# Two lookup layers with 15 of 16 centroid rows in the table products, the spare matrix in a tile of its own

## The chip, the cores and the metric

The kernel runs on one core of one Trainium2 chip. The metric is the device time of one execution in microseconds (us); before, the median of three runs is 3843.47 us (3841.17 to 3844.94). The engines of the core have program counters of their own: TensorE (PE) multiplies matrices and loads weights (PEld), VectorE (DVE), ScalarE (ACT) and GpSimd (POOL) work elementwise, and SyncE (SP) only issues DMAs. They meet through semaphores.

## The reference

Input `x` is 32 images of 1024 channels and 14x14 pixels, fp32. The model's first layer is group norm followed by three lookup layers with batch norm between them; its second is a linear attention with a depthwise convolution. A lookup layer replaces each group of input values by softmax weights over 16 centroids and sums table rows with these weights:

```python
def _amm(patches, centroids, lut, inv_temp):
    ...
    scores = 2.0 * jnp.einsum('blcs,cks->blck', v, centroids) - jnp.sum(centroids * centroids, -1)[None, None]
    attn = jax.nn.softmax(scores * inv_temp, axis=-1)
    out = jnp.einsum('blck,cko->blo', attn, lut)
...
out = _amm(x, c1_centroids, c1_lut, c1_invt)
out = jax.nn.relu(_bn(out, bn1_g, bn1_b))
out = _amm(_extract3x3(out, 1), c2_centroids, c2_lut, c2_invt)
out = jax.nn.relu(_bn(out, bn2_g, bn2_b))
out = _amm(out, c3_centroids, c3_lut, c3_invt)
```

Layers 1 and 2 (the first two lookups) each have 256 codebooks of 16 centroids, so 4096 table rows, and 256 output channels. The 16 weights of a codebook add up to 1. A table whose rows have all had one row of the codebook subtracted gives outputs that differ by a constant per channel, and the batch norm that follows removes such a constant.

## The kernel before

The images go in 16 pairs of 392 tokens. Layers 1 and 2 run over 128 units each: 16 pairs times 8 blocks of 32 codebooks. A unit's weights lie in a tile `t` of 128 partitions by 4 matrices `j` by 416 columns, of which 392 are tokens; a matrix holds 8 codebooks of 16 rows. `units` (L624) is the loop of both layers. Iteration i issues, in this order, the scores and exponentials of unit i + ahead, the 32x32 transposes of the unit before it (`token_major`, L564), `softmax` of unit i + 2 (L576), whatever `side` has for this iteration, and the table products of unit i (`lut`, L631). `ahead` is 4 in layer 1 and 3 in layer 2, and `ahead + 2` tiles `t` go round.

For a unit, PE computes four scores (L779; in layer 2 eight, L896 and L905, from patches and from the padded image), ACT exponentiates them into `t` (L557), DVE transposes `t` into `tt` (L569), in layer 1 Pool first adds the two halves of the 16 (L572), DVE sums (L586), inverts (L588) and transposes back into `r` (L594), Pool multiplies `t` by `r` (L595), and PE multiplies the unit's four matrices by the two halves of the output channels (eight products, L639), adding up over the eight units of a pair in PSUM. Each product is two records in the profile (fp32).

The order of each engine's instructions is that of the program: the whole part stands in a manual schedule. SP issues in order too. It loads in layer 1 the images (L247, a pair 17 iterations ahead of its eight units) and, at the start, eight tables of 512 KB (L237), nine small constants (L182) and the centroids of layers 2 and 3 (L518, L531, L536). A DMA takes one of eight semaphores in turn and is not issued before the last DMA on that semaphore has landed. In layer 2, ACT normalises a pair into `pad` (L813), SP stores it to DRAM three times shifted (`h1d`, L824), and loads for each group of four units 12 patch pieces (L844, `load_patches`, 4 matrices by 3 taps), a group ahead, all at the group's first unit. The tables of layer 2 are loaded as the last units of layer 1 leave their places, and those of layer 3 likewise.

The group norm of a coming pair stands in `side` of layer 1: sums on DVE (L271), means on PE (L281), and a power on Pool (L299).

A second copy of the layers, `layers(True)`, is run only where sums overflow; it is not executed with these inputs.

Of the kernel before, what the change touches and what calls it, by code (L numbers as in the profile page):

```python
# [150 lines left out]
def conv_preact_kernel(ctx: ExitStack, tc: tile.TileContext, a: dict, out: bass.AP):  # L151
# [207 lines left out]
    def score_biases(ps_tr, pool, tmp, i, raw, rows, groups, mask, per, order=None):  # L359
# [44 lines left out]
    lut1_rows = lambda b: a["lut1"][b * 512 : (b + 1) * 512].rearrange("(s q) w -> q s w", q=P)  # L404


    lut2_rows = lambda b: a["lut2"].rearrange("(h j b q) w -> h b q j w", h=2, j=4, q=P)[
        b // 4, b % 4
    ]
# [78 lines left out]
    def layers(exact, early=None):  # L488
# [87 lines left out]
        def softmax(pool, u, t, tt, tv):  # L576

            tf = t.rearrange("p j n -> p (j n)")
            n = tf.shape[1]
            if exact:  # L580
                mx = pool.tile([P, n // KC], F32, tag="mx", name="mx", bufs=1)
                nc.vector.tensor_reduce(mx, tv, AX.X, ALU.max)
                nc.vector.tensor_tensor(tv, tv, bc(mx, 2, KC), ALU.subtract)
                nc.scalar.activation(tt, tt, AF.Exp)
            sm = pool.tile([P, n // KC], F32, tag="sm", name="sm")
            nc.vector.tensor_reduce(sm, tv, AX.X, ALU.add)  # L586
            rc = pool.tile([P, n // KC], F32, tag="rc", name="rc")
            nc.vector.reciprocal(rc, sm)  # L588
            if exact:
                nc.vector.tensor_tensor(tv, tv, bc(rc, 2, KC), ALU.mult)  # L590
                nc.vector.transpose(tf, tt)
                return
            r = pool.tile([P, n], F32, tag="r", name="r")
            nc.vector.transpose(r, bc(rc, 2, KC))  # L594
            nc.gpsimd.tensor_tensor(tf, tf, r, ALU.mult)  # L595
            nc.scalar.activation(sm, sm, AF.Copy, accum_out=added[:, u : u + 1])  # L596
# [26 lines left out]

        def units(ahead, ts, pool, luts, score, bias, dst, stats, side, last, halve=False):  # L624
# [6 lines left out]
            def lut(u):  # L631
# [5 lines left out]
                order = [(h, j) for h in range(2) for j in range(4)]  # L637
                for h, j in order if b == 7 else sorted(order, key=lambda k: k[1]):
                    nc.tensor.matmul(  # L639
                        po[h],  # L640
                        luts[b][:, j, h * P : (h + 1) * P],
                        ts[u % len(ts)][:, j, :N2],
                        start=(b == 0 and j == 0),
                        stop=(b == 7 and j == 3),
                    )
# [6 lines left out]
            for i in range(-ahead, n):  # L652
# [8 lines left out]
                if 0 <= u < n:  # L661
                    softmax(pool, u, ts[u % len(ts)], *tts.pop(u))
# [12 lines left out]
        with ExitStack() as s:  # L675
# [55 lines left out]
            luts2 = []  # L731

            def next_lut(b):
                return lambda: luts2.append(load_lut(b, lut2_rows(b)))
# [5 lines left out]
            at(40, masks2)  # L740
            for b in range(7):
                at(8 * (NP - 1) + b + 1, next_lut(b))
# [3 lines left out]
            luts = [load_lut(b, lut1_rows(b)) for b in range(8)]  # L746
            if not exact:
                masks()
                load_consts(True)
            for i in (2, 3):  # L750
                load_raw(i)
            load_raw2()
# [20 lines left out]
            def score1(u):  # L773
# [13 lines left out]
                luts,  # L787
# [8 lines left out]
            next_lut(7)()  # L796
# [3 lines left out]
        with ExitStack() as s:  # L800
            once = s.enter_context(tc.tile_pool(name="p2c", bufs=1))
            st = s.enter_context(tc.tile_pool(name="p2tt", bufs=1 if exact else 2))
            luts, luts3 = luts2, []
# [33 lines left out]
            def load_patches(n, b0=0, m=4):  # L837
                p, h = divmod(n, 2)
                for j in range(4):
# [10 lines left out]

            store_pair(0, 0)
# [34 lines left out]
            def score2(u):  # L886
# [3 lines left out]
                if g == 0 and n + 1 < 2 * NP:  # L890
                    load_patches(n + 1)
# [24 lines left out]
            def side2(i):  # L916

                p = {1: 1}.get(i + ahead, (i + ahead + 9) / 8)
                if p in range(1, NP):
                    for h in range(2):  # L920
                        store_pair(int(p), h)
                if i == 60:
# [5 lines left out]
            def next_lut3(b):  # L928
# [10 lines left out]
                luts,  # L939
# [888 lines left out]
```

## Time and profile before

| what | value |
|---|---|
| median of three runs | 3843.47 us |
| the profiled execution, its own time | 3843.16 us |
| its span | 3841.0 us |
| PE busy | 3721.5 us, 97% |
| DVE busy | 3001.9 us, 78% |
| POOL busy | 2302.9 us, 60% |
| ACT busy | 1688.2 us, 44% |
| table products of layers 1 and 2 (L639) | 4096 records, 1417.9 us |
| first and last table product of layer 1 | start at 40.0, end at 860.5 us |
| first and last table product of layer 2 | start at 895.2, end at 1897.8 us |

Busy times are of one execution. The group lines give line, engine, operation, output and input, count, busy time, mean length of one in ns, and the idle time before them with what ended it. A window's line gives, for a stretch of the span, its length and each engine's busy time with the number of instructions, then PE's clock, the busy share of the DMA engines, and GB/s. A timeline's line gives start, length, engine, line, operation and tiles.

### The profile page before, as it was taken

What the parts mean: (1) busy time and instruction counts of PE and PEld (TensorE: products, weight loads), DVE (VectorE), ACT (ScalarE), POOL (GpSimd) and SP (SyncE); (2) the same over time, 40 slices, a digit from 0 to 9 for tenths busy, and PEclk for the clock granted to TensorE, in tenths of its full rate; (3) what the DMA queues carried; (4) which work ended last, traced back from release to release, by engine and by line L of the source; (5) the groups of instructions that cost most, each with busy time, mean ns of one, the idle gap of its engine ahead of it and who ended that gap; (6) DMA issues with size and microseconds to landing.
All of it is one profiled execution on the core that took longest, in us unless ns stands there. A gap on an engine that the chain in (4) does not pass through costs nothing. (4 is left out here: it accounts for less than half of the span.)

```text
span 3841.0 us, 45969 instructions
## 1 busy us (share of the span) xinstructions
PE 3721.5 (97%) x16467; PEld 2085.5 (54%) x16467; DVE 3001.9 (78%) x4281; ACT 1688.2 (44%) x3851; POOL 2302.9 (60%) x1338
## 2 busy tenths in 40 slices
PE   8999999999999999999999999998999999999998
PEld 5555555554555545555444444444666666666665
DVE  8999999978888888888733333332699999999996
ACT  4555555533333333333212221121766776667764
POOL 6999999974444444444321111111788888878886
PEclk9999999999999999999999999999999999999999
DMA  3111101015343424343111110012222223322221
GB/s 117 34 35 34 33 19 34 17 45 121 67 96 71 92 53 94 70 91 74 44 39 47 39 39 26 32 39 97 65 79 84 83 85 91 85 81 84 83 80 34
DMA packets 219107, 243.17 MB, mean 63 GB/s; under 512 B 24368, under 2 KB 216752, under 8 KB 218872
## 3 DMA queue, kind: packets, MB, share of 16 engines
q1 hardware_dynamic: 218296, 240.02, 23.4%
q8 instruction: 132, 2.16, 0.3%
q14 instruction: 103, 0.84, 0.1%
q10 hardware_dynamic: 576, 0.15, 0.0%
HBM read 163.55 MB, written 76.56 MB: 63 GB/s over the span
## 5 line engine op out<-in xcount | busy, mean ns | idle before, releaser
L595 POOL TENSOR_TENSOR t<-t,r 128x1664 f32<-128x1664 f32 (+1 forms) x284 | 1064.5, 3748 | 1187.9 <-DVE r L594 1150.7
L639 PE MATMUL po<-t,lut 128*128 128x392 f32 x4096 | 1417.9, 499 | 0.5 <-POOL t L595 0.5
L639 PEld LDWEIGHTS po<-t,lut 128*128 128x128 f32 x4096 | 759.7, 190 | 626.7 <-issue 123.2
L557 ACT ACTIVATE t<-sc,cbias 128x392 f32<-128x392 f32 (+1 forms) x1136 | 579.8, 593 | 1031.6 <-PE sc L905 646.2
L1338 PE MATMUL mm<-y,lut 128*128 128x392 f32 x2048 | 717.4, 497 | 3.4 <-DVE q L1355 3.2
L1004 PE MATMUL po<-t,lut 128*128 128x448 f32 x1792 | 682.2, 541 | 1.7 <-issue 1.7
L569 DVE STREAM_TRANSPOSE tt<-t 128x1664 f32<-128x1664 f32 (+1 forms) x284 | 544.3, 1916 | 168.1 <-ACT t L557 167.9
L594 DVE STREAM_TRANSPOSE r<-rc 128x1664 f32<-128x1664 f32 (+1 forms) x284 | 546.6, 1925 | 21.3 <-DVE rc L588 0.9
L1560 DVE SCALAR_TENSOR_TENSOR pa<-y,lepe_w,pa 128x406 f32<-128x406 f32 x900 | 541.2, 637 | 19.4 <-PE pa L1542 16.3
L1004 PEld LDWEIGHTS po<-t,lut 128*128 128x128 f32 x1792 | 339.1, 190 | 341.6 <-issue 341.4
L1338 PEld LDWEIGHTS mm<-y,lut 128*128 128x128 f32 x2048 | 373.3, 189 | 253.5 <-issue 10.6
L1013 DVE BATCH_NORM_STATS2 stats<-o 128x6 f32<-128x448 f32 x112 | 68.9, 617 | 487.5 <-ACT o L1012 487.5
L586 DVE TENSOR_REDUCE sm<-tt 128x104 f32<-128x832 f32 (+2 forms) x284 | 423.1, 1490 | 5.4
L572 POOL TENSOR_TENSOR tt<-tt 128x832 f32<-128x832 f32 x128 | 248.1, 1939 | 7.8 <-DVE tt L569 7.8
L1012 ACT COPY o<-po 128x448 f32<-128x448 f32 x112 | 59.0, 528 | 425.4 <-PE po L1004 381.1
L588 DVE RECIPROCAL rc<-sm 128x104 f32<-128x104 f32 (+1 forms) x284 | 229.5, 808 | 9.8
L896 PE MATMUL sc<-patch,cw 64*128 64x392 f32 x1024 | 211.9, 520 | 3.8 <-DMA patch<-h1d 2.4
L596 ACT ACTIVATE sm<-sm 128x104 f32<-128x104 f32 (+1 forms) x284 | 86.1, 303 | 177.2 <-DVE rc L588 177.0
L1523 POOL TENSOR_TENSOR qr<-qr,zb 128x784 f32<-128x784 f32 x64 | 117.8, 1852 | 65.5 <-DMA zb<-zd 65.3
L896 PEld LDWEIGHTS sc<-patch,cw 64*128 64x128 f32 x1024 | 90.5, 186 | 116.2 <-issue 73.7
L1347 ACT ACTIVATE e<-mm,kbd 128x392 f32<-128x392 f32 x128 | 74.3, 580 | 167.0 <-PE mm L1338 165.8
L1191 ACT ACTIVATE w<-x,tb,gn_a 128x196 f32<-128x196 f32 x248 | 128.2, 517 | 29.0 <-DVE x L1205 13.0
(179 smaller groups left out, 3996.4 us busy)
## 6 DMA issues: line engine op xcount, KB each, us to landing
patch<-h1d SPq DMA_DIRECT2D x248, 162.8 KB
x<-in_x_dram SPq DMA_DIRECT2D x32, 784.0 KB
o3d<-o SPq DMA_DIRECT2D x14, 1792.0 KB
x<-in_x_dram SPq DMA_DIRECT2D x64, 392.0 KB
out_dram<-x SPq DMA_DIRECT2D x64, 392.0 KB
o<-o3d SPq DMA_DIRECT2D x62, 392.0 KB
h1d<-pad SPq DMA_DIRECT2D x96, 225.0 KB
patch<-h1d SPq DMA_DIRECT2D x124, 108.5 KB
```

What stands on the lines that cost most here:

```text
L557: nc.scalar.activation(t[:, j, : sc.shape[1]], sc, AF.Identity if exact else AF.Exp, bias=bias[:, j : j + 1],)
L569: nc.vector.transpose(tt, tf)
L572: nc.gpsimd.tensor_tensor(tv[:, :, :8], tv[:, :, :8], tv[:, :, 8:], ALU.add)
L586: nc.vector.tensor_reduce(sm, tv, AX.X, ALU.add)
L588: nc.vector.reciprocal(rc, sm)
L594: nc.vector.transpose(r, bc(rc, 2, KC))
L595: nc.gpsimd.tensor_tensor(tf, tf, r, ALU.mult)
L639: nc.tensor.matmul(po[h], luts[b][:, j, h * P : (h + 1) * P], ts[u % len(ts)][:, j, :N2], start=(b == 0 and j == 0), stop=(b == 7 and j == 3),
L896: nc.tensor.matmul(sc, w8[r, 8 * h + 4 * (j // 2) + g], grid(pbuf[n % NPB][r, j // 2, g]), start=True, stop=False,)
L1004: nc.tensor.matmul(po, luts[g][:, m * P : (m + 1) * P], t3[h][:, g % 4, :], start=(g == 0), stop=(g == 7),)
L1338: nc.tensor.matmul(pv(), w[kt][:, m0 : m0 + P], ywin(p, first + kt), start=(kt == 0), stop=(kt == 3),)
L1560: nc.vector.scalar_tensor_tensor(acc, neighbours(p, c, offset(k)), lw[:, c, k : k + 1], acc, ALU.mult, ALU.add,)
```

## The change

In layers 1 and 2 a group of four units has 16 matrices. The first matrix of the group's first unit is the spare one: it is no longer multiplied. In the other 15, the last row of each codebook is given up (`packed_lut`, `last_rows`): Pool subtracts the codebook's last table row from the whole table block (`less`), and the freed places, partitions 15, 31, ..., 127, take rows of the spare matrix, table and weights alike (15 matrices times 8 places for 8 codebooks times 15 rows). `softmax` writes the spare matrix to a tile `spares` of 128x392, by a second multiplication on Pool, and `spare_rows` copies its rows by DMA, 8x392 each, into `t`: three copies for the first unit of a group, four for each other.

The table is loaded as before (`own`), then its 8 foreign rows (`others`), and into a second tile `d` the last rows, each broadcast over its codebook's 16 places, with the foreign codebooks' last rows at their places. In layer 1 `d` is room in `out1` that is not yet written; in layer 2 it is one of two tiles `drop`, whose next load follows the subtraction. The subtractions of layer 1 stand in iterations -3 to 4, with the loads of a block one to three iterations earlier; in layer 2 they stand in iterations -2 to 5, each with its last foreign load just before it and the load for two blocks later just after.

The small constants and the centroids of layers 2 and 3, loaded at the start before, move to iteration 16 of layer 1 (`later`). `load_patches` issues 6, 3 and 3 pieces at the first three units of a group in place of 12 at the first.

```diff
--- before.py
+++ after.py
@@ -401,12 +401,50 @@
         return bias, biases
-    lut1_rows = lambda b: a["lut1"][b * 512 : (b + 1) * 512].rearrange("(s q) w -> q s w", q=P)
-    lut2_rows = lambda b: a["lut2"].rearrange("(h j b q) w -> h b q j w", h=2, j=4, q=P)[
-        b // 4, b % 4
-    ]
+    lut1_tiles = a["lut1"].rearrange("(b j c k) w -> b j c k w", j=4, c=8, k=KC)
+    lut2_tiles = a["lut2"].rearrange("(h j b c k) w -> h b j c k w", h=2, j=4, c=8, k=KC)
+    def unit_rows(layer, b):
+        return lut1_tiles[b] if layer == 1 else lut2_tiles[b // 4, b % 4]
+    def packed_lut(layer, b):
+        rows, spare = unit_rows(layer, b), unit_rows(layer, b - b % 4)[0]
+        j0 = 0 if b % 4 else 1
+        k0 = 4 * (b % 4) + j0 - 1
+        v = weights[b].rearrange("p (s w) -> p s w", s=4)
+        def own():
+            nc.sync.dma_start(v[:, j0:], rows[j0:].rearrange("j c k w -> (c k) j w"))
+        def others():
+            nc.sync.dma_start(v[15::16, j0:], spare[:, k0 : k0 + 4 - j0])
+        return v, own, others
+    def last_rows(d, layer, b):
+        rows, spare = unit_rows(layer, b), unit_rows(layer, b - b % 4)[0]
+        j0 = 0 if b % 4 else 1
+        v = weights[b].rearrange("p (s w) -> p s w", s=4)
+        d = d.rearrange("p (s w) -> p s w", s=4)
+        for j in range(j0, 4):
+            nc.sync.dma_start(d[:, j], rows[j][:, 15:].to_broadcast([8, KC, W]))
+        def others():
+            nc.sync.dma_start(d[15::16, j0:], spare[:, 15:].to_broadcast([8, 4 - j0, W]))
+        def less():
+            nc.gpsimd.tensor_tensor(v[:, j0:], v[:, j0:], d[:, j0:], ALU.subtract)
+        return others, less
     sums = cp.tile([P, 3], F32, tag="sums", name="sums")
     sc3 = cp.tile([P, CT], F32, tag="sc3", name="sc3")
@@ -573,7 +611,8 @@
                 tv = tv[:, :, :8]
             return tt, tv
-        def softmax(pool, u, t, tt, tv):
+        def softmax(pool, u, t, tt, tv, spare=None):
             tf = t.rearrange("p j n -> p (j n)")
             n = tf.shape[1]
@@ -592,6 +631,9 @@
                 return
             r = pool.tile([P, n], F32, tag="r", name="r")
             nc.vector.transpose(r, bc(rc, 2, KC))
+            if spare is not None:
+                nc.gpsimd.tensor_tensor(spare, tf[:, :N2], r[:, :N2], ALU.mult)
+                tf, r = tf[:, NCP:], r[:, NCP:]
             nc.gpsimd.tensor_tensor(tf, tf, r, ALU.mult)
             nc.scalar.activation(sm, sm, AF.Copy, accum_out=added[:, u : u + 1])
@@ -621,6 +663,22 @@
                 ts.append(t)
             return ts
+        spares = [
+            (dram if exact else big).tile([P, N2], F32, tag=f"spare{exact}{k}", name=f"spare{k}")
+            for k in range(2)
+        ]
+        def spare_rows(ts, u):
+            q = u % 4
+            t, kept = ts[u % len(ts)], spares[u // 4 % 2]
+            if exact and q == 0:
+                nc.sync.dma_start(kept, t[:, 0, :N2])
+            for j in range(0 if q else 1, 4):
+                nc.sync.dma_start(t[15::16, j, :N2], kept[4 * q + j - 1 :: 16])
         def units(ahead, ts, pool, luts, score, bias, dst, stats, side, last, halve=False):
@@ -634,13 +692,14 @@
                     po[:] = [
                         ps_po.tile([P, 512], F32, tag="po", name="po")[:, :N2] for h in range(2)
                     ]
-                order = [(h, j) for h in range(2) for j in range(4)]
+                j0 = 0 if b % 4 else 1
+                order = [(h, j) for h in range(2) for j in range(j0, 4)]
                 for h, j in order if b == 7 else sorted(order, key=lambda k: k[1]):
                     nc.tensor.matmul(
                         po[h],
                         luts[b][:, j, h * P : (h + 1) * P],
                         ts[u % len(ts)][:, j, :N2],
-                        start=(b == 0 and j == 0),
+                        start=(b == 0 and j == j0),
                         stop=(b == 7 and j == 3),
                     )
                 if b == 7:
@@ -659,7 +718,14 @@
                     tts[u] = token_major(pool, ts[u % len(ts)], halve)
                 u = u - 1 if halve else u
                 if 0 <= u < n:
-                    softmax(pool, u, ts[u % len(ts)], *tts.pop(u))
+                    softmax(
+                        pool,
+                        u,
+                        ts[u % len(ts)],
+                        *tts.pop(u),
+                        spare=spares[u // 4 % 2] if u % 4 == 0 else None,
+                    )
+                    spare_rows(ts, u)
                 while late:
                     nc.vector.bn_stats(*late.pop(0))
                 side(i)
@@ -728,28 +794,55 @@
                 for r in range(0, 3 * W, P):
                     nc.sync.dma_start(v[r : r + P, : LEAD + 1], zl)
-            luts2 = []
-            def next_lut(b):
-                return lambda: luts2.append(load_lut(b, lut2_rows(b)))
+            luts2 = [packed_lut(2, b) for b in range(8)]
             for p in range(NP):
                 for c in range(CT):
                     at(8 * p + c - AHEAD - 1 - (p == 0), normalise(p, c))
             at(24, edges)
             at(40, masks2)
+            for b in range(8):
+                if b > 1:
+                    at(b - 6, lambda b=b: load_last(b))
+                    at(b - 5, lambda b=b: others(b))
+                at(b - 3, lambda b=b: lasts[b][1]())
+            def later():
+                if not exact:
+                    load_consts(True)
+                for i in (2, 3):
+                    load_raw(i)
+                load_raw2()
+            at(16, later)
             for b in range(7):
-                at(8 * (NP - 1) + b + 1, next_lut(b))
+                at(8 * (NP - 1) + b + 1, luts2[b][1])
+                if b < 6:
+                    at(8 * (NP - 1) + b + 2, luts2[b][2])
             for p in range(2):
                 xts[p] = load_x(xp, p)
-            luts = [load_lut(b, lut1_rows(b)) for b in range(8)]
+            luts = [packed_lut(1, b) for b in range(8)]
+            lasts = []
+            def load_last(b):
+                d = out1[:, b // 4, NTOK - (b % 4 + 1) * C :][:, :C]
+                lasts.append(last_rows(d, 1, b))
+            def others(b):
+                luts[b][2]()
+                lasts[b][0]()
+            for b in range(2):
+                luts[b][1]()
+                load_last(b)
+            for b in range(2, 8):
+                luts[b][1]()
+            for b in range(2):
+                others(b)
             if not exact:
                 masks()
-                load_consts(True)
-            for i in (2, 3):
-                load_raw(i)
-            load_raw2()
             bias1, biases = score_biases(ps_tr, once, st, 1, raw[1], P, CT, mask8, 4)
             w1 = score_matrices(once, 1, "", raw[1], mask8)
             gn = [
@@ -784,7 +877,7 @@
                 AHEAD,
                 unit_tiles(once, AHEAD),
                 st,
-                luts,
+                [v for v, *_ in luts],
                 score1,
                 bias1,
                 out1,
@@ -793,14 +886,25 @@
                 lambda h: bn_final(once, stats1, 1, [h], sc1, bi1),
                 halve=not exact,
             )
-            next_lut(7)()
+            luts2[7][1]()
             add_up(0, 8 * NP)
         with ExitStack() as s:
             once = s.enter_context(tc.tile_pool(name="p2c", bufs=1))
             st = s.enter_context(tc.tile_pool(name="p2tt", bufs=1 if exact else 2))
-            luts, luts3 = luts2, []
+            luts3 = []
+            lasts = []
+            def load_last(b):
+                if b < 8:
+                    t = st.tile([P, C], F32, tag="drop", name="drop", bufs=2)
+                    lasts.append(last_rows(t, 2, b))
+            def without_last(b):
+                lasts[b][0]()
+                lasts[b][1]()
+                load_last(b + 2)
             for k in (2, 3):
                 t = once.tile([P, 2 * IMG], F32, tag=f"pad{k}", name=f"pad{k}")
@@ -834,9 +938,9 @@
                 for k in range(NPB)
             ]
-            def load_patches(n, b0=0, m=4):
+            def load_patches(n, b0=0, m=4, js=range(4)):
                 p, h = divmod(n, 2)
-                for j in range(4):
+                for j in js:
                     for r0, dy, k in TAPS:
                         g0 = 16 * h + 4 * j + b0
                         r0 += 64 * (j % 2)
@@ -848,6 +952,7 @@
                             ),
                         )
+            luts2[6][2]()
             store_pair(0, 0)
             load_patches(0, 0, 1)
             load_patches(0, 1, 3)
@@ -887,8 +992,8 @@
                 p, b = divmod(u, 8)
                 h, g = divmod(b, 4)
                 n = 2 * p + h
-                if g == 0 and n + 1 < 2 * NP:
-                    load_patches(n + 1)
+                if g < 3 and n + 1 < 2 * NP:
+                    load_patches(n + 1, js=((0, 1), (2,), (3,))[g])
                 grid = lambda v: v.rearrange("p (i r c) -> p i r c", r=15, c=15)[:, :, :14, :14]
                 scs = [scores(N2) for j in range(4)]
                 for j, sc in enumerate(scs):
@@ -919,6 +1024,13 @@
                 if p in range(1, NP):
                     for h in range(2):
                         store_pair(int(p), h)
+                if i == -ahead:
+                    luts2[7][2]()
+                    for b in range(2):
+                        load_last(b)
+                for b in range(8):
+                    if i == max(b - 2, 1 - ahead):
+                        without_last(b)
                 if i == 60:
                     bias3, biases = score_biases(ps_tr, big, st, 3, raw[3], P, 2, mask8, 4)
                     parts[3] = score_matrices(big, 3, "", raw[3], mask8), bias3
@@ -936,7 +1048,7 @@
                 ahead,
                 unit_tiles(once, ahead),
                 st,
-                luts,
+                [v for v, *_ in luts2],
                 score2,
                 bias2,
                 out2,
```

## The prediction

> **What bounds the kernel now.** I read the page's busy time by slice first (PE at 9 tenths through both layers), then the stage windows, the longest groups, and the timelines of DVE and SP at the seams. The two stretches are layer 1 and layer 2 in steady state.
>
> ```profile
> core 0: us, PE busy (x) PEld busy (x) DVE busy (x) ACT busy (x) POOL busy (x), PEclk, DMA share, GB/s
> 400.00:600.00 200.00, 200.00 (x775) 104.72 (x774) 192.54 (x221) 102.00 (x256) 186.21 (x71) 1.00 0.11 33
> 1400.00:1600.00 200.00, 200.00 (x814) 100.80 (x814) 170.09 (x111) 64.82 (x165) 95.60 (x26) 1.00 0.38 80
> ```
>
> PE is full in both, but in layer 1 DVE (96%) and Pool (93%) stand right behind it; in layer 2 DVE is at 85%, Pool at 48%. The groups that the change touches:
>
> ```profile
> L595 POOL TENSOR_TENSOR t<-t,r 128x1664 f32<-128x1664 f32 (+1 forms) x284 | 1064.5, 3748 | 1187.9 <-DVE r L594 1150.7
> ...
> L639 PE MATMUL po<-t,lut 128*128 128x392 f32 x4096 | 1417.9, 499 | 0.5 <-POOL t L595 0.5
> ```
>
> Pool's product is the last thing a table product waits for, and PE hardly waits (0.5 us in all), though Pool itself waits 1151 us for DVE's r. A table product is two records; the records of a unit start 0.329 us apart in the trace, so one product is 0.658 us. A layer-1 unit on PE is 0.87 (scores) + 5.46 = 6.33 us, eight units with group norm 51.6; a layer-2 unit is 7.853.
>
> How fast DVE could go alone is seen where it is still catching up with PE, units 8 to 16:
>
> ```profile
> 94.77 1.91 DVE L594 STREAM_TRANSPOSE r<-rc 128x1664 f32<-128x1664 f32 x1
> 96.60 0.99 DVE L664 BATCH_NORM_STATS2 stats<-out 128x6 f32<-128x392 f32 x2
> 97.51 0.16 DVE L295 TENSOR_SCALAR gve<-gn_ps 128x16 f32<-128x16 f32 x1
> 97.59 1.90 DVE L569 STREAM_TRANSPOSE tt<-t 128x1664 f32<-128x1664 f32 x1
> 99.41 0.98 DVE L586 TENSOR_REDUCE sm<-tt 128x104 f32<-128x832 f32 x1
> 100.42 0.80 DVE L588 RECIPROCAL rc<-sm 128x104 f32<-128x104 f32 x1
> 101.26 1.91 DVE L594 STREAM_TRANSPOSE r<-rc 128x1664 f32<-128x1664 f32 x1
> ```
>
> No gap. By this timeline r of unit 8 starts at 83.05, of unit 16 at 132.87: 49.8 us per eight units is DVE's floor. The last view is what SP issues, the small loads at the start and one patch set of layer 2:
>
> ```profile
> 28.09 11.90 SPq L531 DMA_DIRECT2D craw<-in_c_dram  x16
> ...
> 1404.00 6.84 SPq L844 DMA_DIRECT2D patch<-h1d  x12
> ```
>
> **What the Trainium skill says.** "TensorE: Matmul & The Clock Gate", the "Engine queue depth" row of its opening table: LDWEIGHTS is pulled ahead of matmuls in flight. The trace agrees: semaphore waits of the next scores stand in PE's queue during a table stream without changing the 0.329 us spacing. So a row's wait that is already met costs nothing. Its "What's actually happening": an idle window of about 3.4 us halves the clock. At layer 2's start eight score records take 1.69 us, later 0.94. "DMA: Bandwidth & Descriptors", "Why a DMA increments its semaphore": the engines used divide both slowest dimensions, so 8-row copies use 8 engines; the 8-row loads of L531 show eight data landings, the last 2.03 us after issue.
>
> **The change, part by part.**
>
> *Products removed.* Two of 32 per four units: 1.316 us per group, 64 groups, 84 us of PE. Layer 2 becomes 7.853 − 0.329 = 7.524 per unit and stays PE-bound (DVE 6.6). In layer 1, PE needs 51.6 − 2.63 = 48.9 per eight units, below DVE's 49.8: only 1.8 of the 2.63 can be had.
>
> *Spare tile.* Pool at 1664 elements takes 3.68 us start to start, at 832 1.89: 2.15 ns per element plus 0.10. 392 + 1248 instead of 1664 is 0.04 more; Pool then needs 47.9 per eight units, hidden by DVE.
>
> *Rows by DMA.* 15 copies of 8x392 per four units. One-row patch loads are issued every 0.41 us and land 1.8 after issue, so the first rows land 1.85 after Pool's product. In layer 1 the loop r(u) → product 3.87 → rows 1.85 → table 5.46 → scores, exponentials 3.1 → transpose of u+5 is 14.3 of three DVE iterations (18.7): 4.4 us of cover. Behind an x load (lands 6.7 after its second issue) rows lose 2; covered. In layer 2, product end to table start is 10.80 us now, 9.5 to 10.8 after. Worst place: after the six h1d stores SP issues six patch loads; in before the sixth lands 13.5 us after the first store, so the next unit's rows land at about +15.3 where PE wants them at +17.35. Covered by 2 us. That the patch loads are in three portions is what keeps it so; the last portion lands 7 us before its scores.
>
> *Table corrections in layer 1.* A subtraction on 128x1024 is 0.10 + 2.20 = 2.30 on Pool (768: 1.75), in iterations −3 to 4. Pool then needs 3.68 + 1.89 + 2.30 per unit, more than DVE. Stepping through: subtraction 0 fits behind the first halving (32.1 to 33.8), product 0 ends at 40.0 as before; then subtraction 1 to 42.3, halving 2 to 44.2, product 1 to 47.9 where it was 46.2, and so on. Products end at 40.0, 47.9, 55.8, 63.7, 74.3 (after a group norm), 82.2, 90.1, 98.0, 103.6 for units 0 to 8, where unit 8's ended at 88.9. DVE takes over at unit 9, whose r ends at 104.2 instead of 91.2: 13 us late.
>
> *Late constants.* Nine small loads, two raw, 16 of L531 and two of L536 move to iteration 16 on SP: 3.9 + 0.8 + 11.4 + 1.3 = 17.4 us. Queued behind them are unit 19's rows: due 6.2 us after unit 18's product, issued after 1.75 + 17.4, landing at +20.9 instead of +8.1. PE waits 12.8, loses some 2.3 more while cold (an estimate: one window or a little over at half clock), and the transpose of unit 24 waits for those scores: 12.8 + 2.3 − 4.4 ≈ 10.9 lost by DVE.
>
> *Layer 1 summed.* r(115) = 104.2 + 106/8 × 49.8 + 10.9 = 775. From there no group norm is left and PE bounds: table 115 at 780.7, eight units at 48.0 → 828.8 for unit 123, the last four 25.2: 854.0, where before ends at 860.5. Gain 6.5.
>
> *Table corrections in layer 2.* Here "others", subtraction and the next broadcast stand in one iteration, so they form a chain: Pool product 3.72, SP wakes 0.1, four row issues 1.64, the correction's 8-row load 2.03, 0.1, subtraction 2.30 = 9.9 per unit, where PE needs 7.85. Queued behind a blocked SP are the broadcast for b+2 (its buffer is freed by the subtraction) and the next patches. Start: SP first issues six patches, seven broadcasts (128 KB each), three patches, three rows, six h1d stores; the first correction lands at about 904, subtraction 0 ends at 906 (product 0 had ended at 888.9). Following units: 10.9, 9.9, 12.6 (behind six patches), 10.4, 10.9, 15.4 (behind the stores), 9.9: sum 80, so unit 7's table starts at 986 instead of 950.2, 36 late. The 30 groups that follow give back 30 × 1.316 = 39.5. Gain 3.5.
>
> Sum: 3843.2 (the profiled execution's own time; span 3841.0 plus 2.2 around it) − 6.5 − 3.5 = 3833. The median of the runs is 0.3 higher: 3834.
>
> **Bounds of what before does not show.** SBUF-to-SBUF rows: landing 1.5 (the zl stores) to 3.6 us (the first L531 loads, while others are in flight); I take 1.8, the one-row patches; at 3.6 the layer-2 chain is untouched (the correction load is issued later), the worst unit loses nothing yet. The in-place subtraction: 1.89 (halving-like, strided) to 2.6. The layer-2 chain per unit: 9 to 14 us, a delay of 20 to 60. Burst of constants: fully covered (0) to 15 us. Gain from leaving out the row waits on PE: none below zero.
>
> **Rivals.**
> *Corrections hidden (faster).* If Pool's idle half in layer 2 absorbs them and loads land early, the delay there is some 10 us instead of 36: 3808. For it: Pool at 48%. Against: SP and Pool wait for each other in strict order.
> *Layer-2 chain longer (slower).* Place: first eight units of layer 2; price: 7 × what a unit takes beyond 11.4. It decides once the unit's mean passes 14 us (36 + 18 = 54 lost against 46 gained and 7.7 measurable); at 16 us, 3866. For it: patches, stores and broadcasts share the rings with the correction load; PE goes cold in the gaps.
> *Rows late in steady layer 2.* If the worst unit's rows come 4 us later than I have it, 2 us × 15, and with the patch portions twice that: 3834 + 30 = 3864 or more.
> *Layer 1 gains nothing.* If the three engines at 98% each do not interleave, eight units stay at 51: 3834 + 13 = 3847, no change.
>
> **How the numbers follow.** Own forecast 0.46 (3834, its range 3820 to 3848); corrections hidden 0.12; longer chain 0.18; rows late 0.11; layer 1 without gain 0.13. What this kernel's measurement can tell from no change is 0.2%, 7.7 us. The forecast's own mass is split about 0.28 faster, 0.16 same, 0.02 slower; with the rivals: faster 0.40, same 0.28, slower 0.32. The range 3806 to 3868 leaves out the ends of both.
>
> **What would show it.** Table-product records 3840 instead of 4096. Layer 1's windows with DVE at 99% and PE at 97 to 98%; its table products waiting for row DMAs around unit 19 by some 13 us, once. Layer 2's first eight units at 10 to 15 us each with Pool waiting for the correction's load, then 7.52 us per unit with no wait on rows. Wrong if PE waits for rows at each eighth unit of layer 2, if unit 7 of layer 2 starts its table under 20 or over 50 us late, or if layer 1 runs eight units in more than 50.5.

## The result and the profile after

The changed kernel takes 3855.2 us (median of six runs, 3851.4 to 3859.6), beside 3843.0 us for the kernel before (six runs, 3839.5 to 3844.9): a ratio of 1.0034, with a 95% interval of 1.0021 to 1.0047. The forecast was 3834; the change is slower by 12 us. The profiled execution after took 3854.55 us with a span of 3852.8.

The windows of three stretches of after (columns as before), and below them the stretch of before in which its layer 2 starts:

```profile
core 0: us, PE busy (x) PEld busy (x) DVE busy (x) ACT busy (x) POOL busy (x), PEclk, DMA share, GB/s
400.00:600.00 200.00, 196.60 (x771) 102.17 (x769) 197.19 (x225) 108.67 (x266) 192.29 (x81) 1.00 0.14 41
900.00:1000.00 100.00, 59.10 (x196) 27.96 (x196) 51.11 (x32) 17.43 (x45) 38.23 (x15) 0.79 0.42 102
1400.00:1600.00 200.00, 194.42 (x796) 97.19 (x793) 173.41 (x122) 65.77 (x167) 94.68 (x33) 0.98 0.38 83
```

```profile
900.00:1000.00 100.00, 100.00 (x412) 50.12 (x411) 86.88 (x56) 33.29 (x84) 49.98 (x14) 1.00 0.38 87
```

In the middle of layer 1, VectorE now leads (98.6%) and PE follows (98.3%). From 900 to 1000 us, where layer 2 starts, PE works 59% of the time at a clock of 0.79, where before it worked all of it: that is the hole. The table products' group and the waits that end on the new parts (in us: total, times, longest):

```profile
L698 PE MATMUL po<-t,lut 128*128 128x392 f32 x3840 | 1346.7, 504 | 64.2 <-POOL lut L445 33.4
```

```profile
POOL lut L445 <- DMA drop<-in_lut_dram: 51.6, 5, 15.5
PE po L698 <- POOL lut L445: 33.4, 6, 12.0
PE po L698 <- DMA t<-spare: 30.6, 8, 11.6
```

256 records fewer, and 71 us less of table products; but these waited 0.5 us in all before and now wait 64, half of it for Pool's subtraction (L445) and half for the row copies (L680, `t<-spare`). Pool in turn waited 51.6 us for the last rows to land.

Pool at the start of layer 2, in its timeline (idle time before the instruction and its releaser in brackets):

```profile
893.46 2.83 POOL L637 TENSOR_TENSOR t<-t,r 128x1248 f32<-128x1248 f32 x1
911.78 1.80 POOL L445 TENSOR_TENSOR lut<-lut,drop 128x768 f32<-128x768 f32 x1 [15.50 <-DMA drop<-in_lut_dram]
913.54 3.70 POOL L637 TENSOR_TENSOR t<-t,r 128x1664 f32<-128x1664 f32 x1
926.12 2.34 POOL L445 TENSOR_TENSOR lut<-lut,drop 128x1024 f32<-128x1024 f32 x1 [8.88 <-DMA t<-spare]
928.42 3.72 POOL L637 TENSOR_TENSOR t<-t,r 128x1664 f32<-128x1664 f32 x1
```

Each product (L637) stands behind the subtraction of the unit before it, and the subtraction behind a load. The profile names a row copy for the second wait, but in the trace all eight subtractions start 0.07 to 0.16 us after their unit's last correction load (L442, the last rows of the foreign codebooks) has landed. They start 13.7 us apart on average (911.8 to 1007.8), where PE needs 7.52 for a unit. In layer 1, PE's timeline has three waits of 5 us and more for rows; these are the products of units 0, 2 and 19:

```profile
46.06 6.50 PE L698 MATMUL po<-t,lut 128*128 128x392 f32 x12 [5.06 <-DMA t<-spare]
...
69.68 7.95 PE L698 MATMUL po<-t,lut 128*128 128x392 f32 x16 [9.92 <-DMA t<-spare]
...
191.17 6.95 PE L698 MATMUL po<-t,lut 128*128 128x392 f32 x16 [11.62 <-DMA t<-spare]
```

Set side by side, by the start of a unit's first table product in the profiled executions (us from the span's start; "tail" runs from the first product of the last eighth of the attention's L1549 products, L1437 before, to the end of the last engine):

| | L1 unit 9 | unit 19 | unit 127 | L2 unit 0 | unit 7 | unit 15 | unit 127 | tail | end |
|---|---|---|---|---|---|---|---|---|---|
| before | 100.3 | 164.5 | 855.3 | 895.2 | 950.1 | 1013.0 | 1892.5 | 130.8 | 3841.0 |
| after | 114.7 | 191.2 | 857.2 | 913.6 | 1010.2 | 1070.4 | 1913.5 | 120.5 | 3852.8 |
| later by | 14.4 | 26.7 | 2.0 | 18.5 | 60.1 | 57.4 | 21.0 | −10.2 | 11.7 |

Three things happen. Layer 1 starts late, catches up, and ends 2 us later than before. Layer 2 is 60 late at unit 7 and gets 39 back. And the attention's tail, which the change doesn't touch, is 10 us shorter, which hides half of the loss. The last had to be explained first.

### The profile page after: what moved, and what is told of

It reads as the page before. It is cut to its first block, busy times and chain, and to the rows that moved or that the text cites. A ratio compares the mean times of both kernels' runs of the same rounds, so it can differ in the third digit from the quotient of the medians.

```text
span 3852.8 us, 49359 instructions
## 1 busy us (share of the span) xinstructions
PE 3661.6 (95%) x16211; PEld 2043.1 (53%) x16211; DVE 2982.0 (77%) x4281; ACT 1699.0 (44%) x3851; POOL 2340.2 (61%) x1418
## 5 line engine op out<-in xcount | busy, mean ns | idle before, releaser
L637 POOL TENSOR_TENSOR t<-t,r 128x1664 f32<-128x1664 f32 (+2 forms) x284 | 1007.1, 3546 | 981.8 <-DVE r L633 715.2
L698 PE MATMUL po<-t,lut 128*128 128x392 f32 x3840 | 1346.7, 504 | 64.2 <-POOL lut L445 33.4
L698 PEld LDWEIGHTS po<-t,lut 128*128 128x128 f32 x3840 | 717.3, 192 | 663.9 <-issue 143.7
L1116 PEld LDWEIGHTS po<-t,lut 128*128 128x128 f32 x1792 | 339.5, 191 | 342.2 <-issue 341.9
L1001 PE MATMUL sc<-patch,cw 64*128 64x392 f32 x1024 | 217.4, 525 | 13.9 <-DMA patch<-h1d 11.8
L1494 POOL TENSOR_TENSOR kr<-k,cosq 128x784 f32<-128x784 f32 x64 | 104.2, 1628 | 54.3 <-DVE k L1471 42.5
```

The source lines that it names most:

```text
L698: nc.tensor.matmul(po[h], luts[b][:, j, h * P : (h + 1) * P], ts[u % len(ts)][:, j, :N2], start=(b == 0 and j == j0), stop=(b == 7 and j = ...
L1001: nc.tensor.matmul(sc, w8[r, 8 * h + 4 * (j // 2) + g], grid(pbuf[n % NPB][r, j // 2, g]), start=True, stop=False,)
L1116: nc.tensor.matmul(po, luts[g][:, m * P : (m + 1) * P], t3[h][:, g % 4, :], start=(g == 0), stop=(g == 7),)
```

## The experiments

All kernels but the two above have one more edit: the planner that writes out the attention stage (`Plan.write`) went through `engines = {p[0] for p in self.pieces}`, a set of names. Python doesn't fix the order of such a set, so it can differ from build to build; where two engines are free at the same moment of the plan, it decides which piece is written first. Orders A and B below fix it.

The expectations count time from points 0.2 to 0.4 us before the span's start; what was measured is told from the span's start. The runs were taken on three chips: e1 to e4, e5 to e8 and e9 to e12 each on one. The kernel before, run beside each of the three sets, had medians of 3845.1, 3844.7 and 3844.0 us.

### Does the build's order move the attention? (e1, e2, e3)

```diff
-        engines = {p[0] for p in self.pieces}
+        engines = ("PE", "DVE", "ACT", "POOL", "SP")     # order A: e1 (before), e2 (after)
+        engines = ("SP", "POOL", "ACT", "DVE", "PE")     # order B: e3 (before)
```

> The kernel before, with nothing changed but that the planner that writes out the attention stage goes through its engines in a fixed order (PE, DVE, ACT, POOL, SP) instead of the order of a set of names, which can differ from one build to the next. Both theories: layers 1 and 2 end as in the kernel before (last table product of layer 2 at 1897 us of the trace, within 2). Theory 1 (the written order moves the attention stage): its total may differ from the 3843 of the kernel before by up to 10 us. Theory 2 (the change itself shortened the attention stage): within 3 us of 3843.

> The changed kernel with the same fixed order. Theory 1: 20 to 24 us slower than e1, as far apart as the two kernels are at the end of layer 3 (+22.8 in their traces); the 12 that was measured is 22 less some 10 that came with another written order. Theory 2: 12 us slower than e1, with the attention stage some 10 us shorter than e1's.

> The kernel before with the fixed order turned round (SP, POOL, ACT, DVE, PE); the plan, its costs and its due times are the same. Theory 1: attention stage 5 to 15 us away from e1's, layers 1 to 3 within 2 us of e1's. Theory 2: total within 3 us of e1.

Measured: e1 3844.8 us, e2 3870.1, e3 3834.0. The ratios to the kernel before are 1.0002 (0.9993 to 1.0011), 1.0081 (1.0064 to 1.0098) and 0.9970 (0.9959 to 0.9981). The same program in order B is 11 us faster than in order A, and in one order the change costs 25 us by the medians (e2's four runs lie between 3866.7 and 3879.9), 19 by the two profiled executions. The tail in the windows, first of e1, then of e3, then of the changed kernel as it was built:

```profile
3717.90:3846.40 128.50, 111.76 (x748) 74.84 (x744) 95.24 (x184) 65.47 (x145) 87.10 (x75) 0.95 0.12 40
```

```profile
3714.40:3835.00 120.60, 108.86 (x748) 73.13 (x746) 89.67 (x187) 65.78 (x147) 88.25 (x76) 0.98 0.15 48
```

```profile
3732.50:3853.10 120.60, 108.74 (x748) 73.00 (x744) 89.63 (x187) 65.77 (x147) 88.14 (x76) 0.97 0.15 48
```

The same 748 PE records take 128.5 us in order A and 120.6 in B. The changed kernel's tail has B's length and its counts (187, 147 and 76 on DVE, ACT and Pool), while e2's tail has order A's (129.2 us; 184, 146, 75). The traces settle the order itself: after layer 3, the kernel before, e1 and e2 have the same sequence of compute instructions and DMA issues on every engine, and the kernel after has that of e3. From layer 3's last table product to the end the first three take 1177.4, 1181.6 and 1181.0 us, the kernel after and e3 1165.7 and 1165.3. So theory 1 holds: about half of what the change lost was hidden by another written order. One part of its expectation for e3 misses: layers 1 to 3 end 5.2 us later than in e1, not within 2, so the 16.3 that order B gains after them (5 to 15 expected) leave 11 in all. From here on everything is compared with e1 and e2, in order A.

### Layer 2: is it Pool's work or its wait? (e4)

```diff
-                    t = st.tile([P, C], F32, tag="drop", name="drop", bufs=2)
+                    n = 1 if b % 4 == 0 else 2
+                    t = st.tile([P, (2 + n) * W], F32, tag=f"drop{n}", name="drop", bufs=n)
...
             def without_last(b):
-                lasts[b][0]()
                 lasts[b][1]()
-                load_last(b + 2)
+                if b > 0:
+                    load_last(b + 2)
+                if b > 1:
+                    lasts[b + 1][0]() if b < 7 else None
...
             store_pair(0, 1)
+            for b in range(3):
+                load_last(b)
+                lasts[b][0]()
...
                 if i == -ahead:
                     luts2[7][2]()
-                    for b in range(2):
-                        load_last(b)
```

> The changed kernel in order A, layer 2's corrections taken apart: a third buffer for the last rows, the last rows of units 0 to 2 loaded before the unit loop, the load of the last rows from the other tiles issued a unit ahead of the subtraction, so that the subtraction finds its rows there; the subtractions stay at the same iterations. Theory 1 (the chain is Pool's wait for loads, 51.6 us in five waits): the table product of unit 7 in layer 2 starts 25 to 45 us earlier than in e2 relative to that of unit 0, and the total is 25 to 45 us below e2. Rival (the chain is Pool's own work and DVE's wait for Pool's subtractions, 8 of 2.3 us and what they hold up): at most 10 us below e2.

Measured: 3840.1 us, ratio to before 0.9994 (0.9986 to 1.0003), 30 below e2. Unit 0 to unit 7 takes 61.2 us instead of 95.7 (55.0 in e1). Unit 0 itself comes 5 later; that this is for the last rows' loads, which now stand among the first patches, was not tried. Pool in e4:

```profile
902.31 3.71 POOL L638 TENSOR_TENSOR t<-t,r 128x1664 f32<-128x1664 f32 x1 [2.87 <-DVE r L634]
905.96 2.35 POOL L446 TENSOR_TENSOR lut<-lut,drop 128x1024 f32<-128x1024 f32 x1
908.85 3.70 POOL L638 TENSOR_TENSOR t<-t,r 128x1664 f32<-128x1664 f32 x1 [0.53 <-DVE r L634]
912.50 2.34 POOL L446 TENSOR_TENSOR lut<-lut,drop 128x1024 f32<-128x1024 f32 x1
```

Where the rows are there, subtraction and product follow each other in 6.5 us, less than a unit of PE. It is mainly the wait, not Pool's work; the rival allowed 10. One long wait is left (18.3 us, for unit 3's last rows): their buffer is free at 908.3, when the subtraction of unit 1 ends, but SP reaches these loads only at 925.8, behind stores, patches and row copies.

### Constants and stores moved (e5)

```diff
-            at(16, later)
+            nc.sync.dma_start = lambda *v: rest.append(v)
+            later()
+            nc.sync.dma_start = real
+            for k, v in enumerate(rest):
+                at(16 + k // 2, lambda v=v: nc.sync.dma_start(*v))
...
-            luts2[6][2]()
             store_pair(0, 0)
...
             store_pair(0, 1)
+            luts2[6][2]()
```

> The changed kernel in order A with two loads moved. Layer 1: the burst of late constants at iteration 16 is spread, two loads an iteration. Layer 2: the spare rows of unit 6's tables are asked for after the first store to DRAM instead of ahead of it. Theory (the rows of units 16 to 19 stand behind the burst on SP, and VectorE, which sets the rate of layer 1, stands still for as long): unit 19 of layer 1 at 178 to 181 instead of 191.5, the last unit of layer 1 9 to 12 earlier than in e2; and from there to unit 0 of layer 2 5 to 8 shorter; together 14 to 19 below e2. Rival (the lateness at unit 19 is given back anyway in the 100 units that follow): the last unit of layer 1 at most 3 earlier.

Measured: 3858.5 us, 1.0042 (1.0028 to 1.0056), 12 below e2, not 14 to 19. The first half holds roughly: unit 19 at 181.6, the last unit of layer 1 8.7 earlier (849.5); PE's wait for rows around unit 19 shrinks from 10.6 to 0.3 us. What VectorE loses in layer 1 is not given back. The second half misses: from the last unit of layer 1 to unit 0 of layer 2 it stays at 56.9 us (56.6 in e2). SP's first store did come sooner after that unit, 9.3 us instead of 12.8, and the first scores from patches 18.5 instead of 19.7; but Pool's first subtraction then waited 17.05 us for its load instead of 15.27: the gain was swallowed by the next wait.

### What holds the starts: subtraction, loads or rows? (e6, e9)

```diff
-            nc.gpsimd.tensor_tensor(v[:, j0:], v[:, j0:], d[:, j0:], ALU.subtract)
+            pass                                           # e6 and e9
...
-            nc.sync.dma_start(d[:, j], rows[j][:, 15:].to_broadcast([8, KC, W]))
+            pass                                           # e9 only
...
-            nc.sync.dma_start(d[15::16, j0:], spare[:, 15:].to_broadcast([8, 4 - j0, W]))
+            pass                                           # e9 only
```

> The changed kernel in order A without the 16 subtractions on Pool, with all of their loads kept (the computation leaves out the subtraction of the last row). Theory of the prediction for layer 1 (the subtractions hold up VectorE): unit 9 of layer 1 at 101 to 105 instead of 114.5. Rival (the row copies stand behind the loads of tables, last rows and x in the rings): unit 9 moves by less than 4. Layer 2: if Pool's wait for the loads is the whole chain, unit 0 to unit 7 takes 55 to 63 instead of 95.7; if the rows behind the loads hold it as well, over 70.

> The changed kernel in order A without any correction: neither the 16 subtractions nor the loads of the last rows for them (the computation leaves out the subtraction); packing, spare matrix, row copies and portions stay. Layer 1: if the loads of the last rows are what stood ahead of the first rows, unit 9 comes at 101 to 106 instead of 114.5; if the row copies stand behind the table and x loads, which stay, it comes at 110 or later. Layer 2, unit 0 to unit 7 (95.7 in e2, 80.3 without the subtractions alone, 55 in e1): 55 to 64 if the remaining 25 are SP waiting for the last rows' loads and the rows behind them; over 72 if the row copies are late by themselves.

Measured: e6 3843.4 us (27 below e2), e9 3801.1 (69 below). Both leave out the subtraction, e9 its loads too. Layer 1's unit 9 stands at 114.3 in e2, at 113.6 without the subtractions, and at 100.1 without the loads too (e1: 100.8). PE's waits from 40 to 110 us, in e2, e6 and e9:

```profile
PE po L698 <- DMA t<-spare: 16.3, 2, 10.7
```

```profile
PE po L698 <- DMA t<-spare: 14.3, 2, 7.7
```

```profile
PE po L698 <- DMA t<-spare: 3.7, 2, 2.2
PE po L698 <- POOL tt L610: 2.4, 1, 2.4
```

So layer 1's start is held by row copies that stand behind the loads of the last rows, and only in small part by Pool's subtractions: at the end of unit 9's `r` on VectorE (91.5 in e1) they are 3.8 us (107.2 in e2, 103.4 in e6) and the loads 11.1 (92.3 in e9). In layer 2, unit 0 to unit 7 takes 95.7, 80.3 (e6) and 56.8 (e9). Taken out in this order, the subtractions are 15.4 us and the loads 23.5; but e4 keeps both and takes 61.2, so what costs is mostly their order, and the parts can't be added up. SP's waits from 890 to 1012 us show how the loads hold it, in after and then in e6:

```profile
SPq L439 <- DMA drop<-in_lut_dram: 16.4, 6, 3.7
SPq L439 <- POOL lut L445: 13.6, 6, 2.5
```

```profile
SPq L439 <- DMA drop<-in_lut_dram: 14.1, 7, 2.7
```

The broadcasts for unit b + 2 (L439) go into the buffer of unit b, so SP stands until b's last load has landed and, in after, until Pool has subtracted; patches and row copies stand behind it. e9 has no such wait. Row copies without these loads are not late in layer 2: e9 is within 2 of e1 there.

### x earlier, patches in one portion (e7)

```diff
-                at(8 * p - 17, load(p))
+                at(8 * p - 17 if p > 2 else -5, load(p))
...
-                if g < 3 and n + 1 < 2 * NP:
-                    load_patches(n + 1, js=((0, 1), (2,), (3,))[g])
+                if g == 0 and n + 1 < 2 * NP:
+                    load_patches(n + 1)
```

> The changed kernel in order A with two loads moved. Layer 1: x of pair 2 is loaded four iterations earlier, before the units. Layer 2: the twelve patch loads of a half in one portion, as in the kernel before, instead of three. Layer 1, theory (rows of unit 2 wait behind the x load): unit 2 at 58 to 64 instead of 70, unit 9 at 105 to 110 instead of 114.5. Rival: unit 0 becomes as much later as unit 2 becomes earlier. Layer 2, theory of the prediction (rows have about 10 us to spare in the steady state): 7.52 us a unit from unit 15 to 127, as in e2, total moved there by less than 3. Rival (the portions keep the rows in time): over 7.55 us a unit, 4 us or more slower there.

Measured: 3946.9 us, 1.0272 (1.0250 to 1.0295), 77 above e2. The early x only moves the wait: unit 2 comes 3.4 earlier (66.5, not 58 to 64), unit 0 6.5 later, unit 9 0.5 later, and layer 1 ends 2.1 later. All else is the portions: from unit 15 to unit 127 of layer 2 it takes 914.8 us, 8.17 a unit, where e2 takes 842.6, 7.52 a unit. My theory expected no more than 3 us there. PE's waits in that stretch of e7, and one of them in its timeline:

```profile
PE po L698 <- DMA t<-spare: 47.3, 11, 6.1
```

```profile
1414.58 7.92 PE L698 MATMUL po<-t,lut 128*128 128x392 f32 x16 [6.14 <-DMA t<-spare]
```

In e2 the same wait sums to 0.2 us. With twelve pieces ahead of them on SP and in the rings (the queues of the DMA engines), the rows miss units 15, 23, and so on, nearly every eighth. The waits are 47 of the 72 us; the rest fits what the late units then lose: the one shown takes 7.92 us where 5.53 is usual, and eleven times this 2.4 is 26. The portions are what makes row copies affordable in layer 2.

### The corrections a pass earlier than they are used (e8, e11, e12)

The first eight units of a layer can use whole tables, 16 products as before, while the corrected ones are prepared; this costs two groups' saving (2.6 us) a layer. In e8 the first pair's outputs keep the constant that the other pairs lack. e11 takes it out: one more column of `t` holds a mask of the last rows, so that the first pass's accumulator sums them, and ScalarE subtracts this column when it copies the accumulator.

```diff
-                j0 = 0 if b % 4 else 1
+                j0 = 0 if b % 4 or p == 0 else 1
+                n2 = N2 if p else N2 + 1                   # e11
...
+                at(b - 1, lambda b=b: load_last(b))        # layer 1
+                at(b, lambda b=b: lasts[b][0]())
+                at(b + 2, lambda b=b: luts[b][2]())
+                at(b + 4, lambda b=b: lasts[b][1]())
...
+                    if i == b + 4:                         # layer 2, e8
+                        lasts[b][1]()
+                    if i == b + 3:
+                        load_last(b)
+                        lasts[b][0]()
...
+                    if i == (3, 4, 5, 7, 9, 8, 10, 11)[b]: # layer 2, e11, with e4's buffers
+                        lasts[b][1]()
...
+                    if i == (0, 1, 2, 5, 7, 6, 8, 9)[b]:
+                        load_last(b)
...
+                    if i == (1, 2, 3, 6, 8, 7, 9, 10)[b]:
+                        lasts[b][0]()
```

> The saving without the start chains, in order A: in both layers the first eight units use all 16 products of the uncorrected tables, as in the kernel before; last rows, spare rows and subtractions of table b come in iterations b-1 to b+4 of that first pass, eight units before they are used; constants and table loads stand where they stand in the kernel before. Theory (what the change lost is the two start chains and the burst): unit 9 of layer 1 within 3 of e1's 101.1; layer 1 ends 4 to 18 before e1's 856.0 (VectorE's rate of 6.22 a unit, less what 8 subtractions of 2.3 us hold it up); layer 2 gives 39.5 by its groups 2 to 31; total 3787 to 3802, 43 to 58 below e1. Rival (subtractions amid the units stall PE just as much wherever they stand): over 3815.

> e8's design, completed: the first pass's accumulators carry one more column, the product with a mask of the last rows, and ScalarE subtracts it when it copies the first pass out, so that all passes lack the same constant; in layer 2 a third buffer, and the last rows asked for at least one iteration ahead of the rows from the other tiles, and these ahead of the subtraction. Theory (e8's loss of 21 us between units 7 and 15 of layer 2 is SP, which stands behind the landing of the last rows in each iteration, and with it rows and patches): unit 7 to unit 15 of layer 2 takes 63 to 70 instead of 84.3; total 3796 to 3804. Rival (Pool's subtraction and product together are too long for a unit): over 78 there, and total over 3812.

> e11 with the attention stage written in order B: the order's gain and the layers' gain stand beside each other, 8 to 14 below e11, 3784 to 3796. Rival (the attention stage's order gains only when it starts at e1's time): within 4 of e11.

Measured: e8 3818.2 us, 0.9936 (0.9920 to 0.9953), 16 above the 3802 expected and past the rival's 3815, though not by the rival's mechanism. Layer 1 ends 12.6 before e1, as expected, but units 7 to 15 of layer 2 take 84.4 us instead of 62.8. SP waits for the broadcasts that it has just issued into the same buffer (L442, from 935 to 1030 us):

```profile
SPq L442 <- DMA drop<-in_lut_dram: 20.4, 10, 4.7
```

e11, with one iteration between them and a third buffer, has no such wait from 935 to 1005 us, with the same subtractions. It takes 62.6 there and 3800.0 in all, 0.9886 (0.9870 to 0.9903): as fast as e9, which does no corrections (but has the burst of constants). e12, in order B, takes 3787.2, 0.9854 (0.9837 to 0.9870). Both e11 and e12 are faster than both kernels. e11's windows, and Pool in layer 1:

```profile
900.00:1000.00 100.00, 97.71 (x404) 48.75 (x403) 87.00 (x56) 33.83 (x88) 67.74 (x25) 1.00 0.54 121
1400.00:1600.00 200.00, 199.71 (x819) 100.14 (x819) 174.73 (x113) 69.52 (x176) 99.85 (x33) 1.00 0.41 87
```

```profile
96.66 3.72 POOL L638 TENSOR_TENSOR t<-t,r 128x1664 f32<-128x1664 f32 x1
100.33 2.36 POOL L446 TENSOR_TENSOR lut<-lut,out 128x1024 f32<-128x1024 f32 x1
102.64 1.93 POOL L611 TENSOR_TENSOR tt<-tt 128x832 f32<-128x832 f32 x1
```

Layer 2 starts without a hole. In layer 1 the subtractions have their own price here: product, subtraction and halving take 7.9 us a unit, and units 9 to 19 take 72.7 us where e1 takes 64.2.

### The least repair (e10)

e4's and e5's first edit together, nothing new.

> The changed kernel in order A with e4's layer 2 and e5's spread constants together. If the two losses stand beside each other: 3830 to 3834, that is 36 to 40 below e2 and 11 to 15 below e1. Rival (what layer 1 gains is lost again in layer 2's first chain, as most of e5's earlier store was): 3836 or more.

Measured: 3825.0 us, 0.9953 (0.9936 to 0.9969), 45 below e2, 20 below e1 and 5 below the range expected. The two losses stand beside each other; it is better than the sum, as layer 1 gains 10.7 here (8.7 in e5) and unit 0 to unit 7 takes 59.2 (61.2 in e4).

## Why the prediction was wrong

*Products removed*: right. After the start of layer 2, the 30 groups come 1.30 us earlier each, 39.1 in all (60.1 late at unit 7, 21.0 at unit 127) against 39.5 forecast, and units run at 7.53 us.

*VectorE's floor in layer 1*: right. From unit 24 to 112 it takes 49.77 us per eight units (forecast 49.8); the rival "layer 1 gains nothing" is out.

*Table corrections in layer 1*: size about right, cause wrong. `r` of unit 9 was forecast to end at 104.2, 13 us late, and ended at 107.2. The step charged the delay to Pool stepping through the subtractions; e6 and e9 charge most of it to row copies behind the last rows' loads. What failed is that "the first rows land 1.85 after Pool's product" and that rows behind an x load lose 2 us: for unit 0 the product ends at 42.2 and the first rows land at 45.9; for unit 2, 57.9 and 69.6. By the end, layer 1 has lost 2.0 in place of gaining 6.5. Of these 8.5 us, 3.0 are there at `r` of unit 9; 2.6 come up to `r` of unit 115 (780.6, forecast 775); and 2.8 between this and unit 115's table product (8.5 us, forecast 5.7). What causes the last two was not tried.

*Late constants*: right. 10.9 us forecast; from unit 9 to 19 it takes 76.5 us, and 64.7 in e5; spreading them brings 8.7 to 10.7 at the end of layer 1 (e5, e10).

*Table corrections in layer 2*: right mechanism, wrong size, and the largest miss. Unit 7 was forecast 36 late, over 50 was to be a sign of being wrong, and it came 60.1, or 58.1 after layer 1's 2.0. The first subtraction ended at 913.6 (911.6 less those 2.0) in place of 906; from there to unit 7's table product it took 96.6 in place of 80. The mis-sized terms are those on SP and in the rings. Four row issues take 2.5 to 2.8 us, once 5.0, not 1.64; and the correction loads let Pool go 2.4 to 4.4 us after their issue starts, 3.3 on average, not 2.03. The Trainium skill, "DMA: Bandwidth & Descriptors", "Queues, rings and completion order", says that on each DMA engine one sequencer's descriptors are consumed in ring order; these runs agree, as the rows of layer 2's start come in time once the loads of the last rows ahead of them are gone (e9). In the trace of after, the last row copy of a unit lands 1.7 us after its issue where little is ahead (at 934 us), and the first of a unit 9.5 us behind six patch pieces (944) and 11.1 us behind broadcasts and an x load (58). From 40 to 110 us no row copy takes more than 5.7 us in e9, which has that x load but no broadcasts, or 4.6 in e7, which has the broadcasts but loads that x earlier.

I had priced each DMA as if the rings were free. The 1.8 us taken for rows is right for the steady state: from 1012 to 1900 us their median is 1.7. From 890 to 1012 us it is 5.5. The trace of before could have warned me: 1.8 is what nine patch pieces at 869 to 872 us take to land, while the median of all 396 is 6.45.

*Rivals.* "Layer-2 chain longer" was to decide the sign beyond 14 us a unit; the mean was 13.7. It fell short alone; with layer 1's 8.5 it made the change slower. I had let no two misses come together. "Corrections hidden" is false for this kernel, but e11 shows that it can be had. "Rows late in steady layer 2" did not happen, and e7 shows how near it was: the portions' two microseconds of cover are worth 72 us, not the 30 that I gave it.

*The sum*: −10 forecast, + 8.5 from layer 1, + 22.1 from layer 2's start: + 20.6, where the profile has + 21.0 at layer 2's last unit. The attention's written order, which no step contained, made the part after layer 3 11.7 us shorter (1165.7 for 1177.4). That the measured time lies within my range is owed to that, so it is luck: in order A the median is 3870.1. Which of the attention's pieces gains the time was not tried.

## What to carry to other kernels

Where a loop can run its first pass in the old form, prepare its data (a correction, a repack) during that pass, a full pass ahead of their first use. Here this hid the preparation of layer 2; in layer 1 it cost 8 us over ten units, and the layer still ended 13.9 us before e1's (847.3 for 861.2). Price a small DMA by what is ahead of it on its issuing engine and in its rings, not by its latency alone (1.7 to 11.1 us for the same row copy here); and after removing one wait, read which one is next before counting the gain (e5). Before crediting a change with a few tenths of a per cent, see that the parts it doesn't touch were written in the same order in both builds.

## What the runs showed that I had not expected

- One program, written in two orders that its planner holds equal, differs by 11 us (0.3%). In the profiles the part after layer 3 differs by 16.3, of which 7.9 are in the attention's tail (128.5 against 120.6 us).
- A row copy of 8x392 inside SBUF holds SP for 0.65 us, where a patch piece takes 0.42 to 0.46; a broadcast of last rows takes 0.64.
- Twelve patch loads in one piece instead of 6, 3 and 3 cost 72 us over 112 units once rows have to get past them. The kernel before has the twelve and no rows, and its PE is busy for all of the 200 us from 1400 to 1600.
